# The last step of two layer norms on ScalarE instead of VectorE and GpSimd, in a kernel of windowed attention and product-key experts

## The chip, the cores and the metric

The kernel runs on one core of a Trainium2 chip. A core has five engines with an instruction queue of their own: PE (TensorE: matmuls and transposes), DVE (VectorE), ACT (ScalarE), POOL (GpSimd) and SP (SyncE, which here only issues DMAs). They run at the same time and wait for each other by semaphores. Each of them works through its queue in the order in which the program was built, so an instruction that waits holds up all those behind it. Tiles live in SBUF, matmul results in banks of PSUM.

The metric is the device time of one execution in microseconds (us). The kernel before took 1505.26 us, the median of 3 runs (1503.28 to 1505.82).

## The reference

The input x has 16 sequences (B) of 512 tokens (T) with 128 channels (D). Two residual layers are computed, each behind a layer norm without weights:

```python
def _layernorm(x, axis=-1, eps=1e-05):
    m = jnp.mean(x, axis=axis, keepdims=True)
    v = jnp.var(x, axis=axis, keepdims=True)
    return (x - m) / jnp.sqrt(v + eps)

x = L0_attn_x
x = x + _L0_attn_ref(_layernorm(x, axis=-1), L0_attn_w_qkv, L0_attn_w_proj)
x = x + _L0_ffn_ref(_layernorm(x, axis=-1), L0_ffn_gamma, L0_ffn_beta, L0_ffn_w_q,
                    L0_ffn_keys, L0_ffn_key_in, L0_ffn_key_out)
```

The attention has 16 heads of 8 channels. A token sees the tokens at most 128 places away:

```python
attn = jnp.einsum('bhqd,bhkd->bhqk', q, k) / math.sqrt(DK)
mask = jnp.abs(idx[None, :] - idx[:, None]) > WINDOW          # 128
p = jax.nn.softmax(jnp.where(mask[None, None], -1000000000.0, attn), axis=-1)
out = jnp.einsum('bhqk,bhkd->bhqd', p, v)                     # then the projection
```

The second layer normalises its input over all 8192 tokens, scores it against 2 x 8 x 32 keys, takes the eight best of each and the eight best of their sums, and weighs 1024 experts by them:

```python
mu, var = jnp.mean(x, axis=0), jnp.mean(jnp.square(x - mu), axis=0)
xn = (x - mu) * jax.lax.rsqrt(var + BN_EPS) * gamma + beta
sim = jnp.einsum('pbnhd,hkpd->pbnhk', (xn @ w_q.T)..., keys)
s, i = jax.lax.top_k(sim, 8)
o = jax.nn.gelu(inputs @ w_down) * jax.nn.softmax(scores, axis=-1)
out = jnp.einsum('bnhk,bnhkd->bnd', o, w_up)
```

## The kernel before

**Two stages.** An attention stage (up to about 716 us) is followed by an expert stage (to the end). The second cannot begin earlier, because its scores need mean and variance over all tokens: `bn_st` collects the statistics of each normalised sequence and L591 joins them. The change touches the attention stage alone.

**Attention.** The unit of work is a unit `n` of one sequence and four heads (64 in all), in four blocks `u` of 128 tokens. The outer loop (L548) runs over steps `s`, one step per (n, u). In a step, PE, DVE, ACT and POOL work on different units:

- `greatest` (L409) is two units ahead: a matmul of q with k into `s_ps` for each head, and on DVE a masked maximum over it (L424, written `masked` and `mx` in the profile). Four times a step. `s_ps` has three PSUM banks.
- `greatest_pieces` (on POOL, tiles `mr` and `mp`) and `greatest_rows` split the maxima into three bf16 pieces, transpose them on PE (`mT_ps`), copy them on ACT and write them by DMA into rows of `qst`, so that the next matmul subtracts them.
- `exponentials` (L453) is the unit itself: a matmul of k with q into `e_ps` for each head, and on ACT `Exp` of it into `pT` (L466). `e_ps` has three banks as well, so a matmul into `e_ps` waits for the Exp of the third one before it. POOL then zeroes the corners outside of the window (`affine_select`, called from L473).
- `weigh` (L479), two steps later: `pT` times v into `o_ps`.
- `divide` and `project` finish a unit and a sequence; L525 adds the result to `xs[b]`, which stays in SBUF for the whole kernel.

**Work beside it.** Three lines of steps run beside this loop, `preparing`, `ending` and `beside`, each a generator (`Steps`, L282). At the end of each step of the loop every line takes at most one step, and one that needs the single PSUM bank `ps_m` (it yields `BANK`) waits for a step in which that bank is free.

- `prepare(b)` (L339) makes q, k and v of a sequence three ahead: `normalised_T` (L320), which normalises the four blocks of 128 tokens into `xn`, transposes them on PE into `xn_ps` and copies them on ACT into `xnT`; then the matmuls, ACT's copies `qf` and `kf`, and POOL's splitting of q and k into bf16 pieces (`qp`, `kp`, `rest`).
- `second_norm(bs)` (L527) is the layer norm ahead of the experts: statistics, then `normalised_T` again with tiles called `xi`, `xi_ps` and `xiT`, and a DMA of `xiT` to DRAM. It runs in groups: sequences 0 to 5, 6 to 11, 12 and 13, 14, and 15 last (L547, L585).
- `ln_stats` (L303) makes the statistics of a group, block by block (`bn_stats` and `bn_aggr` on DVE), one step of the line for each sequence, and at the group's end one `Sqrt` on ACT and one reciprocal on DVE. For the first norm it is called for sequence 0, for 1, for 2 and 3, and for 4 to 15.
- `weights_of_experts` (L188) loads and prepares the experts' weights, behind the statistics of 4 to 15.

**Last step of a norm.** `normalised_T` computes (x - mean) x rstd for each of the four blocks by one instruction with two per-row operands. Of the four, the second and the fourth go to POOL, the others to DVE; for sequences 0 and 1 (first norm) and for the last sequence (second norm) all four go to DVE:

```python
alone = b == B - 1 if tag == "xi" else b < 2
what = (xn[:, t], xs[b][:, t], mv[:, t, 0:1], rstd[:, t : t + 1], ALU.subtract, ALU.mult)
if t % 2 and not alone:
    pool("tensor_scalar", *what)
else:
    nc.vector.tensor_scalar(*what)
```

The profile writes these as `xn<-x,mva,rsa` and `xi<-x,mvb,rsb`, at L330 for DVE and L172 (the helper `pool`) for POOL.

**What sets the order.** Matmuls, transposes and POOL's instructions in the helpers `mm`, `tr` and `pool` stay in the order of the program text. The others (ACT, DVE, memsets, DMAs) are placed by a planner when the program is built, by the costs that it assumes; on the chip each queue then runs in that fixed order. `Exp` and `Sqrt` need different tables on ACT, so a `Sqrt` between `Exp`s has an ACT_TABLE_LOAD on either side. The four square roots of the first norm stand ahead of the first `Exp`; those of the second norm lie among them.

Of the kernel before, what the change touches and what calls it, by code (L numbers as in the profile page):

```python
# [15 lines left out]
AF = mybir.ActivationFunctionType  # L16
ALU = mybir.AluOpType
# [26 lines left out]
def kernel(  # L44
# [13 lines left out]
    nc = tc.nc  # L58
    B, T, D = x.shape
    NH = 16  # L60
    DK = D // NH
    NQ = T // P
# [17 lines left out]
    xs = []  # L80
    for b in range(B):
        t = keep.tile([P, NQ, D], F32, name=f"x_{b}")
# [59 lines left out]
    def load(b):  # L142
        xts[b] = ahead.tile([P, T], F32, tag="xt", name=f"xt_{b}")
        nc.sync.dma_start(xts[b], xT[b])
# [8 lines left out]
    with ExitStack() as at:  # L153
# [12 lines left out]
        def mm(*args, **kw):  # L166

            tc.keep_in_program_order(nc.tensor.matmul(*args, **kw))  # L168

        def pool(op, *args, **kw):  # L170

            tc.keep_in_program_order(getattr(nc.gpsimd, op)(*args, **kw))  # L172

        def tr(out, in_, eye):
            tc.keep_in_program_order(nc.tensor.transpose(out, in_, eye))
# [12 lines left out]
        def weights_of_experts():  # L188

            for v in range(2):  # L190
                nc.sync.dma_start(
                    key_out_sb[v * NP : v * NP + NP], key_out.rearrange("(p c) d -> p c d", c=NC)
                )
            loads = [
                (f"key_in_{i}", key_in[4 * P * i : 4 * P * i + 4 * P].rearrange("(c p) d -> p c d", p=P))
                for i in range(2)
            ]
            loads.append(("keys", keys.rearrange("(c a) k p d -> (a k) c (p d)", c=2)))
            loads += [
                (f"w_q_{i}", w_q[4 * P * i : 4 * P * i + 4 * P].rearrange("(c k) d -> k c d", k=P))  # L200
                for i in range(4)
            ]
            raw = {}

            def fetch(i):
                if i < len(loads):
                    name, src = loads[i]
                    raw[i] = pw.tile([P, 4, D], F32, tag="raw", name=name)
                    dst = raw[i]
                    if name == "keys":  # L210
                        dst = dst.rearrange("q (c p) d -> q c (p d)", p=2)
                    nc.sync.dma_start(dst, src)

            fetch(0)
            fetch(1)
            yield
            yield
            yield BANK
            keysT = fix.tile([P, 2, 2, P], F32, name="keysT")
            for i in range(len(loads)):  # L220
                w = raw.pop(i)
                ps = ps_m.tile([P, 4, P], F32, tag="m", name=f"prep_ps_{i}")
                if i < 3:
                    for c in range(4):
                        tr(ps[:, c], w[:, c], ident)
                else:

                    for c in range(4):
                        s, h = divmod(4 * (i - 3) + c, H)
                        mm(  # L230
                            ps[:, c, 0:NK], lhsT=w[:, c],
                            rhs=keysT[:, h // 4, s, (h % 4) * NK : (h % 4 + 1) * NK],
                            start=True, stop=True,
                        )
                if i < 2:
                    nc.scalar.copy(
                        key_inT[:, :, NP // 2 * i : NP // 2 * i + NP // 2],
                        ps.rearrange("d k (p c) -> d c (k p)", c=NC),
                    )
                elif i == 2:  # L240
                    nc.scalar.copy(keysT.rearrange("p c s k -> p (c s) k"), ps)
                else:
                    s, h = divmod(4 * (i - 3), H)
                    nc.scalar.copy(
                        wsim.rearrange("p (h s k) -> p h s k", s=2, k=NK)[:, h : h + 4, s],
                        ps[:, :, 0:NK],
                    )
                fetch(i + 2)
                yield
                yield BANK if i + 1 < len(loads) else None  # L250
# [25 lines left out]
        pieced, attns, norms = {}, {}, {}  # L276
# [26 lines left out]
        def ln_stats(bs, name, into):  # L303

            n = len(bs) * NQ
            mv = ln.tile([P, n, 2], F32, tag=f"mv{name}{n}", name=f"mv{name}_{bs[0]}", bufs=3)
            for i in range(n):
                st = ln.tile([P, 6], F32, tag="st", name=f"st{name}_{bs[0]}_{i}", bufs=4)
                nc.vector.bn_stats(st, xs[bs[i // NQ]][:, i % NQ])
                nc.vector.bn_aggr(mv[:, i], st)  # L310
                if i % NQ == NQ - 1:
                    yield
            rstd = ln.tile([P, n], F32, tag=f"rs{name}{n}", name=f"rs{name}_{bs[0]}", bufs=3)
            nc.scalar.activation(rstd[:, 0:n], mv[:, 0:n, 1], AF.Sqrt, bias=eps)
            nc.vector.reciprocal(rstd[:, 0:n], rstd[:, 0:n])
            for i, b in enumerate(bs):
                into[b] = mv[:, i * NQ : i * NQ + NQ], rstd[:, i * NQ : i * NQ + NQ]
            yield

        def normalised_T(b, mv, rstd, dst, tag, then=None):  # L320

            xn = w2.tile([P, NQ, D], F32, tag="xn", name=f"{tag}_{b}")
            for t in range(NQ):

                alone = b == B - 1 if tag == "xi" else b < 2
                what = (xn[:, t], xs[b][:, t], mv[:, t, 0:1], rstd[:, t : t + 1], ALU.subtract, ALU.mult)
                if t % 2 and not alone:
                    pool("tensor_scalar", *what)
                else:
                    nc.vector.tensor_scalar(*what)  # L330
                if t % 2:
                    yield BANK if t == NQ - 1 else None
            ps = ps_m.tile([P, NQ, P], F32, tag="m", name=f"{tag}_ps_{b}")
            for t in range(NQ):
                tr(ps[:, t], xn[:, t], ident)
            nc.scalar.copy(dst, ps.rearrange("p t q -> p (t q)"))
            yield then
# [189 lines left out]
        def second_norm(bs):  # L527
            into = {}
            yield from ln_stats(bs, "b", into)
            for b in bs:  # L530
                t = w2.tile([P, T], F32, tag="xiT", name=f"xiT_{b}")
                yield from normalised_T(b, *into[b], t, "xi")
                nc.vector.bn_stats(bn_st[:, b], t)
                nc.sync.dma_start(xT[b], t)
# [7 lines left out]
        preparing, beside, ending = Steps(), Steps(), Steps()  # L542
# [5 lines left out]
        for s in range(-2 * NG * NQ, (NU + 1) * NQ):  # L548
            n, u = divmod(s, NQ)
            b, g = divmod(n, NG)  # L550
            if g == NG - 1 and u == 2 and b + 3 < B:
                preparing.rest()
                preparing.add(prepare(b + 3))
            if u == 0 and g == 1 and b == 0:
                beside.add(ln_stats(range(4, B), "a", norms), weights_of_experts())
            if u == 0 and g == 2 and b in groups:
                beside.add(second_norm(groups[b]))
            if u == 0 and g == 2 and b == B - 1:
                load(0)
                load(1)  # L560
            tops_of = greatest(n + AHEAD, u) if 0 <= n + AHEAD < NU else iter(())
            probs_of = exponentials(n, u) if 0 <= n < NU else iter(())
            next(tops_of, None)
            next(probs_of, None)
            next(tops_of, None)
            if 0 <= s - LATE < NU * NQ:
                weigh(*divmod(s - LATE, NQ))
            together(tops_of, probs_of)
            free = True
            if u == 0 and 0 <= n + AHEAD - 1 < NU:  # L570
                greatest_pieces(n + AHEAD - 1)
            if u == 1 and 0 <= n + AHEAD - 1 < NU:
                greatest_rows(n + AHEAD - 1)
                free = False
            if u == 2 and 0 <= n - 1 < NU:
                divide(n - 1)
                free = False
                if n % NG == 0:
                    ending.add(project(n // NG - 1))
                    ending.go(False)  # L580
            for steps in (preparing, ending, beside):
                free = steps.go(free)
            if u == NQ - 2 and 0 <= n + LAID < NU:
                lay(n + LAID)
# [41 lines left out]
    pe, dve, act, pool = (InOrder(e) for e in (nc.tensor, nc.vector, nc.scalar, nc.gpsimd))  # L626
# [333 lines left out]
    for i in range(NB):  # L960
        b, t = divmod(i, NQ)
# [110 lines left out]
```

## Time and profile before

| | |
|---|---|
| profiled execution | 1506.56 us, of which the span of the instructions is 1504.9 us |
| median of the runs shown | 1505.26 us |
| attention stage | 0 to about 716 us |
| start of attention, to the first `Exp` | 53.7 us |
| granted TensorE clock over the span | 0.984 |
| DVE, xn and xi by L330 | 36 x 499 ns mean, 34 x 482 ns mean |
| POOL, xn and xi by L172 | 28 x 806 ns mean, 30 x 801 ns mean |
| ACT, `Exp` at 384 and at 256 columns | 512 x 489 ns, 512 x 383 ns |
| ACT, table loads in attention | 11 x 1283 ns |

Busy time of an engine is the time in which it ran an instruction of its own. A row such as `A <- B: 8.8, 14, 0.9` in the list of waits says that A sat idle for 8.8 us in total, 14 times, at most 0.9 us, until B was done. In a list in order of time the columns are start and length in us, engine, line, operation, output and inputs with their shapes, how many in a row, and in brackets the idle time ahead and what ended it. `PEld` is the loading of weights into TensorE, beside the matmuls.

### The profile page before, as it was taken

The numbers are of one execution on the slowest core, as the hardware profiler recorded it, in microseconds if no ns is written. First come the engines' busy times: TensorE is split into PE (matmuls) and PEld (weight loads), VectorE is DVE, ScalarE is ACT, GpSimd is POOL, SyncE is SP. The second block draws the span as 40 slices with busy tenths as digits, with TensorE's granted clock in tenths as the row PEclk, the third lists the DMA queues.
The fourth block names the chain that finished last, engine by engine and source line by source line (L and its number), as shares of the span: only waits on it lengthen the run. The fifth ranks groups of instructions, "written<-read, shape, count | busy, mean of one in ns | idle before, by whom it ended". The sixth has DMA issues, their size and how long they took to land.

```text
span 1504.9 us, 48591 instructions
## 1 busy us (share of the span) xinstructions
PE 1395.0 (93%) x16880; PEld 844.1 (56%) x16880; DVE 1315.6 (87%) x7999; ACT 1212.4 (81%) x2596; POOL 1094.5 (73%) x1706
## 2 busy tenths in 40 slices
PE   3999999999999999896789999999999999999997
PEld 1445555544545545443456666666666666666666
DVE  6878888878888887882899999999999999999984
ACT  1577777777777777775889999999999999999963
POOL 8466666777777767563577887788878788788775
PEclk9999999999999999997999999999999999999989
DMA  6233332223333222320000000000000000000000
GB/s 177 86 111 101 102 94 84 85 79 89 92 91 92 86 85 76 101 63 36 10 9 10 9 17 10 16 17 9 16 10 17 17 10 16 10 16 10 10 2 24
DMA packets 53574, 74.96 MB, mean 50 GB/s; under 512 B 5840, under 2 KB 39888, under 8 KB 53200
## 3 DMA queue, kind: packets, MB, share of 16 engines
q1 hardware_dynamic: 52496, 71.59, 16.2%
q8 instruction: 134, 2.20, 0.6%
q14 instruction: 112, 0.92, 0.2%
q10 hardware_dynamic: 832, 0.26, 0.1%
HBM read 49.28 MB, written 20.97 MB: 47 GB/s over the span
## 4 chain that ended last, share of the span: by engine, by line
DVE 47%; PE 3%; issue 1%; ACT 1%; POOL 0%; ACTq 0%; POOLq 0%
DVE idx L624 10%; DVE row L624 9%; DVE place L624 6%; DVE top L624 6%; DVE mine L624 5%; DVE best L624 4%; DVE x_ps L624 3%; DVE num L624 2%; DVE upper L624 1%; PE up_ps L624 1%; DVE zs L624 1%; PE w_ps L624 1%; POOL cols L624 0%; PE dn_ps L624 0%; PE off_ps L624 0%
## 5 line engine op out<-in xcount | busy, mean ns | idle before, releaser
L424 DVE CUSTOM_DVE_ANT_0 masked<-s_ps,band 128x384 bf16<-128x384 f32 (+1 forms) x1024 | 459.1, 484 | 112.2 <-PE s_ps L168 95.7
L466 ACT ACTIVATE pT<-e_ps 128x384 f32<-128x384 f32 (+1 forms) x1024 | 389.4, 436 | 117.5 <-PE e_ps L168 111.1
L172 POOL TENSOR_SCALAR_AFFINE_SELECT pT<-pT 128x512 f32<-128x512 f32 x384 | 239.2, 639 | 188.8 <-ACT pT L466 187.2
L168 PE MATMUL s_ps<-kst,qst 128*128 128x384 bf16 (+1 forms) x1024 | 309.5, 307 | 22.2 <-DMA kst<-kv 11.0
L624 POOL TENSOR_TENSOR cols<-mine,wT 64x512 f32<-64x512 bf16 x256 | 270.0, 1055 | 25.7 <-ACT row L624 7.0
L624 PE MATMUL w_ps<-cols,row 128*64 128x32 f32 x8192 | 260.0, 224 | 13.6 <-POOL cols L624 13.6
L624 PEld LDWEIGHTS w_ps<-cols,row 128*64 128x64 f32 x8192 | 252.1, 139 | 32.3 <-POOL cols L624 27.8
L168 PE MATMUL e_ps<-qst,kst 128*128 128x384 bf16 (+1 forms) x1024 | 228.7, 302 | 13.1 <-ACT pT L466 12.4
L624 POOL TENSOR_TENSOR g<-g,gel 128x512 f32<-128x512 f32 x128 | 163.6, 1278 | 105.5 <-ACT g L624 105.5
L168 PEld LDWEIGHTS <-qst 128*128 128x128 bf16 x1024 | 100.5, 98 | 196.2 <-issue 168.4
L168 PE MATMUL o_ps<-pT,vaug 128*32 128x384 f32 (+1 forms) x2048 | 192.3, 447 | 0.4 <-POOL pT L172 0.4
L624 DVE FIND_INDEX8 idx<-top,sim 128x8 uint32<-128x32 f32 x1024 | 166.2, 185 | 0.0
L624 ACT ACTIVATE row<-off_p,one 128x512 f32<-128x512 bf16 x256 | 165.8, 749 | 0.0
L624 ACT ACT_TABLE_LOAD x122 | 156.5, 1283 | 2.2
L624 DVE TENSOR_TENSOR row<-x_ps,nums_p 128x1024 f32<-128x1024 f32 x128 | 150.0, 1213 | 0.0
L624 PE MATMUL up_ps<-g,key_out_sb 64*128 64x256 f32 (+2 forms) x1152 | 148.0, 384 | 0.0
L624 ACT ACTIVATE off_p<-off_ps 128x512 bf16<-128x512 f32 x256 | 132.4, 602 | 17.0 <-PE off_ps L624 16.8
L624 PE MATMUL dn_ps<-xt,key_inT 128*64 128x256 f32 x1024 | 125.6, 388 | 2.2 <-ACT sim L624 1.4
L168 PEld LDWEIGHTS <-kst 128*128 128x128 bf16 x1024 | 99.9, 98 | 45.4 <-issue 23.9
L624 PE MATMUL off_ps<-p_bf,ident_bf 128*128 128x512 bf16 x256 | 96.6, 377 | 19.7 <-ACT p_bf L624 19.6
L624 PEld LDWEIGHTS dn_ps<-xt,key_inT 128*64 128x64 f32 x1024 | 68.3, 137 | 78.3 <-ACT row L624 41.7
L624 DVE MAX8 top<-sim 128x8 f32<-128x32 f32 x1024 | 106.7, 177 | 2.9 <-ACT sim L624 2.9
(145 smaller groups left out, 2366.5 us busy)
## 6 DMA issues: line engine op xcount, KB each, us to landing
qst<-qv SPq DMA_DIRECT2D x192, 96.0 KB
kst<-kv SPq DMA_DIRECT2D x192, 96.0 KB
qv<-qp SPq DMA_DIRECT2D x16, 384.0 KB
kv<-kp SPq DMA_DIRECT2D x16, 384.0 KB
x<-in_L_attn_x_dram SPq DMA_DIRECT2D x16, 256.0 KB
xT<-xiT SPq DMA_DIRECT2D x16, 256.0 KB
xt<-xT SPq DMA_DIRECT2D x16, 256.0 KB
out_dram<-o_sb SPq DMA_DIRECT2D x16, 256.0 KB
```

Of the source, the lines that this page charges most:

```text
L168: tc.keep_in_program_order(nc.tensor.matmul(*args, **kw))
L172: tc.keep_in_program_order(getattr(nc.gpsimd, op)(*args, **kw))
L424: nc.vector.tensor_tensor_reduce(masked[h][:, 0:w], s, band.rearrange("p u k -> p (u k)")[:, from_u : from_u + w], 1.0, LOWEST, ALU.add, A ...
L466: nc.scalar.activation(pT[:, h, 0:w], e_ps[:, 0:w], AF.Exp)
L624: return lambda *args, **kw: tc.keep_in_program_order(op(*args, **kw))
```

## The change

The last step of both norms is written as x times rstd plus (-mean x rstd), and all four blocks of every sequence go to ACT as `Identity` with a per-row scale and a per-row bias. For the bias, `ln_stats` gets one more DVE instruction at a group's end, which overwrites the means by -mean x rstd. DVE and POOL have no part in that step any more.

`ln_stats` takes a step of its line after every two blocks of 128 tokens where it took one after four, so that a sequence's statistics are two steps.

The first norm's statistics of sequences 4 to 15 are made as two groups, 4 and 5, and 6 to 15, each with its own square root and reciprocal. `weights_of_experts` stays behind them.

```diff
@@ ln_stats @@
-                if i % NQ == NQ - 1:
+                if i % 2:
                     yield
             rstd = ln.tile([P, n], F32, tag=f"rs{name}{n}", name=f"rs{name}_{bs[0]}", bufs=3)
             nc.scalar.activation(rstd[:, 0:n], mv[:, 0:n, 1], AF.Sqrt, bias=eps)
             nc.vector.reciprocal(rstd[:, 0:n], rstd[:, 0:n])
+            nc.vector.scalar_tensor_tensor(
+                mv[:, 0:n, 0], mv[:, 0:n, 0], -1.0, rstd[:, 0:n], ALU.mult, ALU.mult
+            )
@@ normalised_T @@
-                alone = b == B - 1 if tag == "xi" else b < 2
-                what = (xn[:, t], xs[b][:, t], mv[:, t, 0:1], rstd[:, t : t + 1], ALU.subtract, ALU.mult)
-                if t % 2 and not alone:
-                    pool("tensor_scalar", *what)
-                else:
-                    nc.vector.tensor_scalar(*what)
+                nc.scalar.activation(
+                    xn[:, t], xs[b][:, t], AF.Identity, bias=mv[:, t, 0:1], scale=rstd[:, t : t + 1]
+                )
                 if t % 2:
                     yield BANK if t == NQ - 1 else None
@@ loop over steps @@
             if u == 0 and g == 1 and b == 0:
-                beside.add(ln_stats(range(4, B), "a", norms), weights_of_experts())
+                beside.add(ln_stats([4, 5], "a", norms), ln_stats(range(6, B), "a", norms))
+                beside.add(weights_of_experts())
```

## The prediction

> **What bounds the kernel now.** I read the page first, then a table of busy time by stretch, then the waits of PE between 60 and 700 us, then two places in order of time.
>
> The page's engine line, over the whole span:
>
> ```profile
> PE 1395.0 (93%) x16880; PEld 844.1 (56%) x16880; DVE 1315.6 (87%) x7999; ACT 1212.4 (81%) x2596; POOL 1094.5 (73%) x1706
> ```
>
> The edits touch only the attention stage, which ends at about 716 us; the expert stage after it issues the same instructions. Busy us of each engine in 10 us stretches (PE, PEld, DVE, ACT, POOL, then the granted clock):
>
> ```profile
> 320.00:330.00 10.00, 8.44 (x59) 4.86 (x61) 6.72 (x29) 7.63 (x18) 3.44 (x9) 0.83 0.18 51
> ...
> 350.00:360.00 10.00, 10.00 (x89) 5.65 (x89) 8.16 (x36) 7.41 (x19) 8.46 (x17) 1.00 0.25 74
> 360.00:370.00 10.00, 8.43 (x72) 4.66 (x71) 9.61 (x38) 7.17 (x18) 6.74 (x13) 1.00 0.39 118
> ```
>
> PE is full in an ordinary stretch, so attention lasts as long as PE's work and PE's stalls. Work taken from DVE or POOL is worth only the stalls it caused; work given to ACT costs only where PE comes to wait. What PE waited for from 60 to 700 us (total, times, longest):
>
> ```profile
> PE e_ps L168 <- ACT pT L466: 12.4, 6, 3.7
> PE s_ps L168 <- DVE mx L424: 8.8, 14, 0.9
> PE mT_ps L175 <- POOL mp L172: 5.0, 13, 0.6
> PE xi_ps L175 <- POOL xi L172: 1.0, 2, 0.8
> ```
>
> So at most about 10 us can be won from DVE and POOL. The third line isn't theirs: there POOL's chain follows a pT select that had waited for ACT (1.21 us idle at 173.6). A DVE stall and ACT's slack at one place, in order of time:
>
> ```profile
> 360.60 0.38 PE L168 MATMUL e_ps<-qst,kst 128*128 128x256 bf16 x2
> ...
> 360.69 0.59 ACT L336 COPY xiT<-xi_ps 128x512 f32<-128x512 f32 x1
> 360.69 1.92 DVE L330 TENSOR_SCALAR xn<-x,mva,rsa 128x128 f32<-128x128 f32 x2
> ...
> 361.17 0.67 ACT L466 ACTIVATE pT<-e_ps 128x256 f32<-128x256 f32 x2
> ...
> 361.93 0.38 PE L168 MATMUL e_ps<-qst,kst 128*128 128x256 bf16 x2
> ...
> 363.00 0.27 PE L168 MATMUL s_ps<-kst,qst 128*128 128x256 bf16 x1 [0.69 <-DVE mx L424]
> ...
> 365.05 0.32 PE L168 MATMUL s_ps<-kst,qst 128*128 128x384 bf16 x1 [0.88 <-DVE mx L424]
> ```
>
> And a square root in mid-stream, with its two table loads:
>
> ```profile
> 561.16 1.28 ACT L314 ACT_TABLE_LOAD   x1
> ...
> 562.67 0.32 ACT L314 ACTIVATE rsb<-mvb,eps 128x24 f32<-128x24 f32 x1 [0.23 <-DVE mvb L310]
> ...
> 563.00 1.28 ACT L466 ACT_TABLE_LOAD   x1
> 563.02 0.30 DVE L315 RECIPROCAL rsb<-rsb 128x24 f32<-128x24 f32 x1 [0.38 <-ACT rsb L314]
> ...
> 564.73 0.27 PE L168 MATMUL e_ps<-qst,kst 128*128 128x256 bf16 x1 [2.33 <-ACT pT L466]
> ```
>
> **The change, part by part.** It removes 70 TENSOR_SCALAR from DVE (36 xn, 34 xi) and 58 from POOL (28 and 30), and adds 128 Identity activations on ACT, ten small DVE instructions and one square root, which falls ahead of the first Exp. The changed program's order has as many table loads as before, so Identity brings none.
>
> *Price of one Identity.* The costliest ACT groups with pointer operands (busy us, mean ns), and four of the first in order of time:
>
> ```profile
> L624 ACT ACTIVATE row<-off_p,one 128x512 f32<-128x512 bf16 x256 | 165.8, 749 | 0.0
> L624 ACT ACTIVATE xb<-xt,bn_b,bn_a 128x512 f32<-128x512 f32 x16 | 13.0, 814 | 0.9 <-DVE bn_b L598 0.9
> ...
> 1005.24 2.59 ACT L624 ACTIVATE row<-off_p,one 128x512 f32<-128x512 bf16 x4
> ```
>
> The xb row is this very form at 512 columns: 814 ns. pT at 384 and 256 columns takes 489 and 383 ns, 0.83 ns a column, so 128 columns take 814 - 384 x 0.83 = 495 ns. Four of the Relu follow each other in 2.59 us, so the pitch is (2.59 - 0.749)/3 = 0.614, 0.135 below the duration; an Identity has a pitch of 0.36 us and four take 1.44. Ends: 0.17 (the 128x128 COPY, 266 ns, less the 0.1 by which a copy overlaps the next: 360.69 to 361.17 is 0.48 of 0.59) and 0.68 (xb whole). I take 0.36, the same form corrected for width. Together 46 us: ACT goes from 77% to 84% of 60-700 us.
>
> The Trainium skill, "ScalarE: Activation LUTs", section "What ACT_TABLE_LOAD costs", has 186 ns + 0.833 ns a column, 93 ns for each pointer operand and an overlap of 93 ns; an estimate from it is 479 ns, pitch 0.386, and the sum below would be 10.1 in place of 8.8. Its section "Rules for kernel authors" says to do add and mul on VectorE and not on ScalarE, which speaks against this change; that rule is about cost per element, and no row here gives the price of being queued ahead of Exp.
>
> *Bursts of four ahead of Exp.* In the changed order ten blocks have their four Identities between a copy (xiT, as at 360.69) and the next four Exp. e_ps has three banks. The second matmul of the pair at 361.93 started at 362.04 and needs the bank of the first of the pair at 360.60, whose Exp ended at 361.17 + 0.38 = 361.55; PE restarts 0.05 after an Exp. Slack 0.44. With 1.44 us more ahead of that Exp, PE stalls 1.0 us. Ten times: **+10.0** (by the two end pitches four take 0.66 and 2.7, less 0.44: 2.2 and 22.6). Behind PE's stalled matmul stand all its s_ps and o_ps.
>
> *Square roots.* In two of them (24 columns, at 319.5 and 562.7) ACT now goes sqrt, wait, four Identities, table load. The wait is DVE's reciprocal 0.30, the new instruction (about 0.25, between reciprocals of 4 and 24 columns at 0.18 and 0.30) and hand-overs, 0.75 in all. Behind the sqrt everything on ACT is queued, Exp first, and PE already stalls there, so all of 0.75 + 1.44 is added: 2 x 2.19 = **+4.4** (2.8 to 6.9). At the next two (636.2 and 678.8) four Identities stand ahead of the table load, but ACT waited 1.26 and 0.91 us for DVE's statistics, which cover most: +0.2 and +0.55, **+0.75** (0 to 3.3).
>
> *Clock.* After the stall at 319 the clock row reads 0.83 (1.7 us of ten lost); after the equal one at 563 it is 1.00. With stalls twice as long I count one more such loss: **+1.7** (0 to 3.4). The Trainium skill, "TensorE: Matmul & The Clock Gate", Part 1, says that a free-running window of 3.4 us without work halves the clock; by it the 2.3 us stalls are a matter of phase and 4.5 us ones always lose, so the sum stays as it is.
>
> *Single Identities.* Twelve blocks have them one, two, one between Exp pairs. ACT idles 0.17 to 0.6 us before most pairs; one fits, two (0.72) exceed 0.44 by little: **+1.0** (0 to 3).
>
> *Removed from DVE.* The 8.8 us are four places like 360-366 (0.69 + 0.88 each) and six of 0.41, all right behind TENSOR_SCALARs (1.92, or 1.04 us a pair), each longer than the stall: **-8.8** (-8.8 to -6.3). Next late there is ACT, counted above. POOL's 46 us lay in its waits for ACT (180 us).
>
> *Start.* ACT now runs block 1's four Identities before the copy of block 0's xnT (11.54 us before): statistics of blocks 2 and 3 end some 1 us sooner, their square root waits for block 0's Identities to 10.24, four more to 11.87: +0.35. POOL, full from 14.97 to the kp that the DMA at 28.07 waits for, loses an xn (0.81) and gets a memset (0.95) in its place: +0.15. **+0.5** (-0.8 to 1.5). SP's loads of expert weights come later among the qst loads, the same number; wsim was ready at 211 us and is needed at 716: nothing, and PE and ACT steps moved with them are as many.
>
> *End.* Steps of two blocks push one more xi transposition behind the last y_ps. xiT of block 13 takes block 14's place before the table load, block 14's copy goes behind the sqrt, then the last four Identities end at 712.25 where DVE ended at 711.60: +0.65. Ahead of it PE's waits for POOL's xi (0.83) and pT (0.36) go, and oT is no longer behind xiT: -1.5. **-0.8** (-1.5 to +0.7).
>
> Sum: 10.0 + 4.4 + 0.75 + 1.7 + 1.0 - 8.8 + 0.5 - 0.8 = **+8.8 us**. The profiled execution took 1506.56 us, 1.3 above the median; it goes to 1515.3, the median from 1505.26 to **1514.0**.
>
> **Rivals.**
> - *DVE's relief wins (faster).* If an Identity's pitch is a copy's 0.17, four take 0.66: bursts 2.2, square roots 2.8, no more clock loss, singles nothing. With -9.6 and +0.5 the sum is -4.1: 1501.2. It decides below a pitch of 0.19. For it: 16 us of DVE burst vanish where PE waited. Against: the xb and Relu rows.
> - *Slack is larger than one place shows (no change).* Exp pairs that wait 0.6 us for PE elsewhere; a stall of 0.4 a burst gives 4.0 for 10.0: 1508.0.
> - *ACT becomes the bound.* If half the single Identities also stall PE by 0.7 in each of the twelve blocks, 8.4 replaces 1.0: 1521.5. For it: ACT has no gap between oT and mT copies; against: 16% of the stage still idle.
>
> **How the numbers follow.** Forecast 0.61 (alone 1509 to 1519), faster rival 0.16, no change 0.13, ACT bound 0.10. About 0.2%, 3 us, is what a measurement here can tell from no change, so faster 0.16, same 0.13, slower 0.71. The sums of all low and all high ends are 1499 and 1540; 1503 to 1522 leaves out most of the first rival and the top of the last, two in ten.
>
> **What would show it.** Right: Identity near 495 ns; waits of s_ps for DVE mx near nothing; e_ps waiting for pT about 28 us in some sixteen places, those of 1 us behind an xiT copy; PE idle above 4 us at two square roots. Wrong: an Identity below 300 ns, or bursts with no stall behind them, or mT_ps waits that grow past 5 us, since POOL's chain stands behind ACT's pT.

## The result and the profile after

The changed kernel takes 1512.28 us, the median of 20 runs (1506.36 to 1516.22); the kernel before, run beside it, 1504.59 us (20 runs, 1501.97 to 1507.64). The ratio is 1.005, with a 95% interval of 1.0041 to 1.0058: 7.7 us slower, where 8.8 were forecast. The profiled execution took 1510.33 us (span 1508.6), 2 us below its median, and the one of before lay 2 us above its own; so the two traces differ by 3.8 us only; where the rest may lie is said below the table by stretch.

The page's engine line of the changed kernel: DVE and POOL gave up 24 and 49 us, ACT took 46, PE's work is the same.

```profile
PE 1392.5 (92%) x16880; PEld 842.0 (56%) x16880; DVE 1291.2 (86%) x7940; ACT 1258.6 (83%) x2725; POOL 1045.9 (69%) x1648
```

What PE waited for from 60 to 700 us in the changed kernel (total, times, longest; all rows). The row of `s_ps` for DVE's `mx` has gone whole, and the row of `e_ps` for ACT's `pT` has grown from 12.4 to 27.7 us.

```profile
PE e_ps L168 <- ACT pT L466: 27.7, 17, 4.6
PE mT_ps L175 <- POOL mp L172: 5.8, 16, 0.6
PE s_ps L168 <- DMA qst<-zeros: 1.5, 1, 1.5
```

Busy time by stretch (PE, PEld, DVE, ACT, POOL, then the granted clock, the DMA share and GB/s). PE was full from 350 to 370 us but for its waits for DVE; now it loses 0.94 us there to ACT. After the first square root the clock is 0.83 as before; in the stretch of the second, where it had been 1.00, it is 0.73.

```profile
320.00:330.00 10.00, 8.17 (x58) 4.59 (x61) 5.04 (x20) 7.62 (x18) 3.18 (x9) 0.83 0.05 18
350.00:360.00 10.00, 10.00 (x91) 5.66 (x88) 8.03 (x38) 7.41 (x19) 8.44 (x17) 1.00 0.24 73
360.00:370.00 10.00, 9.06 (x79) 5.05 (x81) 8.69 (x41) 8.92 (x24) 5.70 (x12) 1.00 0.39 120
560.00:570.00 10.00, 5.41 (x31) 3.09 (x29) 4.33 (x24) 7.47 (x16) 3.89 (x9) 0.73 0.29 88
```

One of the ten bursts, in order of time, at the place that the prediction showed of before. The four Identities run in one go behind the `xiT` copy, the next Exp starts at 362.79 in place of some 1.5 us earlier, and PE's matmul into the bank that this Exp frees waits 0.94 us.

```profile
360.67 0.38 PE L168 MATMUL e_ps<-qst,kst 128*128 128x256 bf16 x2
360.76 0.59 ACT L336 COPY xiT<-xi_ps 128x512 f32<-128x512 f32 x1
...
361.24 1.65 ACT L328 ACTIVATE xn<-x,mva,rsa 128x128 f32<-128x128 f32 x4
...
362.00 0.27 PE L168 MATMUL e_ps<-qst,kst 128*128 128x256 bf16 x1
...
362.79 1.18 ACT L466 ACTIVATE pT<-e_ps 128x256 f32<-128x256 f32 x4
...
363.21 0.27 PE L168 MATMUL e_ps<-qst,kst 128*128 128x256 bf16 x1 [0.94 <-ACT pT L466]
```

And the second square root in mid-stream. Between the root and the load of Exp's table stand the wait for DVE (0.59) and the four Identities; PE idles 4.56 us where it idled 2.33.

```profile
560.70 1.28 ACT L314 ACT_TABLE_LOAD   x1
...
562.20 0.32 ACT L314 ACTIVATE rsb<-mvb,eps 128x24 f32<-128x24 f32 x1 [0.22 <-DVE mvb L310]
562.54 0.30 DVE L315 RECIPROCAL rsb<-rsb 128x24 f32<-128x24 f32 x1 [0.38 <-ACT rsb L314]
562.88 0.18 DVE L316 SCALAR_TENSOR_TENSOR mvb<-mvb,rsb 128x24 f32<-128x24 f32 x1
563.10 1.65 ACT L328 ACTIVATE xi<-x,mvb,rsb 128x128 f32<-128x128 f32 x4 [0.59 <-DVE mvb L316]
564.77 1.28 ACT L466 ACT_TABLE_LOAD   x1
...
566.50 0.37 PE L168 MATMUL e_ps<-qst,kst 128*128 128x256 bf16 x1 [4.56 <-ACT pT L466]
```

At the third and the fourth root the stalls grew by little, because ACT's wait for DVE's statistics covers most of the four Identities there. First before, then after:

```profile
638.22 0.27 PE L168 MATMUL e_ps<-qst,kst 128*128 128x256 bf16 x1 [3.68 <-ACT pT L466]
...
680.80 1.07 PE L168 MATMUL e_ps<-qst,kst 128*128 128x256 bf16 x3 [3.66 <-ACT pT L466]
```

```profile
642.53 0.27 PE L168 MATMUL e_ps<-qst,kst 128*128 128x256 bf16 x1 [3.98 <-ACT pT L466]
...
687.69 1.07 PE L168 MATMUL e_ps<-qst,kst 128*128 128x256 bf16 x3 [4.31 <-ACT pT L466]
```

The 64 transpositions into `mT_ps`, one a unit, are marks at which two traces can be laid side by side. After minus before, by stretch (times of before):

| stretch | what lies in it | change, us |
|---|---|---|
| 0 to 57.4 | start | -2.3 |
| 57.4 to 312.8 | single Identities, loads of expert weights | +0.3 |
| 312.8 to 335.8 | first root | +2.0 |
| 335.8 to 556.0 | six bursts against nine waits for DVE | -0.5 |
| 556.0 to 577.4 | second root | +4.3 |
| 577.4 to 627.9 | two bursts against three waits for DVE | +0.15 |
| 627.9 to 670.8 | third root, two bursts | +2.2 |
| 670.8 to 683.8 | fourth root | +0.6 |
| 683.8 to 716.3 | end, to the experts' first `sim_ps` | -3.1 |

So the bursts and DVE's relief cancel almost exactly in the long middle, and the roots are the loss. In the row of the second root 2.2 of the 4.3 us are the longer wait; the clock lost 3.4 us more there (one minus the granted share, summed over 4 us windows), part of it while PE stood still. The two negative rows at the ends lie where the clock was lost in the profile of before: 3.4 us between 40 and 60 us, where after lost nothing, and 6.8 against 1.7 between 700 and 724 us. At the start x also arrived 0.56 us earlier in the second profile. That these make up the two rows is likely, not shown. From 60 to 700 us all rows of PE's waits add up to 35.0 us after and 28.3 before, 6.7 us more, next to the 7.7 of the medians.

### The profile page after: what moved, and what is told of

Read it like the earlier page. It is cut to its first block, busy times and chain, and to the rows that moved or that the text cites. A ratio compares the mean times of both kernels' runs of the same rounds, so it can differ in the third digit from the quotient of the medians.

```text
span 1508.6 us, 48606 instructions
## 1 busy us (share of the span) xinstructions
PE 1392.5 (92%) x16880; PEld 842.0 (56%) x16880; DVE 1291.2 (86%) x7940; ACT 1258.6 (83%) x2725; POOL 1045.9 (69%) x1648
## 4 chain that ended last, share of the span: by engine, by line
DVE 48%; PE 38%; ACT 6%; POOL 4%; issue 2%; DMA 2%; SPq 1%; POOLq 0%; ACTq 0%
DVE idx L625 10%; PE o_ps L168 10%; PE s_ps L168 9%; DVE row L625 9%; PE e_ps L168 8%; DVE place L625 6%; DVE top L625 6%; DVE mine L625 5%; DVE best L625 4%; DVE x_ps L625 3%; ACT pT L466 2%; DVE num L625 2%; PE t_ps L175 2%; PE mT_ps L175 1%; DVE upper L625 1%
## 5 line engine op out<-in xcount | busy, mean ns | idle before, releaser
L168 PE MATMUL e_ps<-qst,kst 128*128 128x384 bf16 (+1 forms) x1024 | 230.5, 302 | 28.4 <-ACT pT L466 27.7
```

## Experiments

Each kernel was timed in several rounds beside the kernel before, which took 1505.0 to 1505.8 us in these jobs. Theory A is that of the prediction: an instruction on ACT costs what it makes the next Exp late by, less a slack.

**Which part of the change: e1 and e2.** The steps undone, or done alone:

```diff
 # e1: the changed kernel, with
-                if i % 2:
+                if i % NQ == NQ - 1:
                     yield
-                beside.add(ln_stats([4, 5], "a", norms), ln_stats(range(6, B), "a", norms))
-                beside.add(weights_of_experts())
+                beside.add(ln_stats(range(4, B), "a", norms), weights_of_experts())
 # e2: the kernel before, with the same lines the other way round
```

> The changed kernel with its step changes undone: statistics yield once a block and blocks 4 to 15 are one group, ahead of the expert weights, as before; the norms' last step is still Identity on ACT. Theory A (what I predicted from: the Identities queued ahead of Exp cost the time, DVE's relief gives 8.8 us back, the steps are worth next to nothing): the order of ACT has the same ten fours behind an xiT copy and the same four behind a square root, so e_ps waits for pT about 27 us between 60 and 705 us, s_ps for DVE mx near nothing, and the 1.5 us wait for the load of qst from zeros at 132 us is gone, since the expert weights are loaded where they were before: about 1511 us (1508 to 1513). Rival B (the finer steps and the later loads of the expert weights lose the time, Identity is even): 1504 to 1506 us, as the kernel before.

> The kernel before with the step changes alone: statistics yield every two blocks of 128, blocks 4 and 5 are a group of their own, and the expert weights come behind all statistics; the norms' last step stays a TENSOR_SCALAR on DVE and POOL. Theory A: s_ps waits for DVE mx stay near 8.8 us and e_ps for pT near 12.4 us; added is the 1.5 us wait for qst from zeros near 132 us: about 1506 us (1503.5 to 1508). Rival B (the steps and the moved loads are the loss): 1510 to 1513 us.

e1 took 1514.18 us, ratio 1.0054 (1.0041 to 1.0068); e2 1505.64 us, ratio 1.000 (0.9989 to 1.0011). The waits from 60 to 700 us, first of e1, then of e2:

```profile
PE e_ps L168 <- ACT pT L466: 27.0, 15, 4.6
PE mT_ps L175 <- POOL mp L172: 5.8, 16, 0.6
PE s_ps L168 <- DMA qst<-mT: 1.3, 1, 1.3
...
```

```profile
PE e_ps L168 <- ACT pT L466: 12.9, 7, 3.7
PE s_ps L168 <- DVE mx L424: 8.8, 14, 0.9
PE mT_ps L175 <- POOL mp L172: 5.8, 15, 0.6
PE s_ps L168 <- DMA qst<-mT: 1.7, 1, 1.7
...
```

The whole loss is Identity's. The finer steps move one wait for `qst` from 112 us (0.6 to 1.3 us long in the six profiles with the old steps) to about 140 us (1.5 to 2.1 in seven of the eight with the new; e3 has no such wait), and the time does not show it.

**Price and slack: e5 and e6.** Two Identities in place of four, and eight.

```diff
 # e5: the changed kernel, with
+                if t % 2:
                     nc.scalar.activation(xn[:, t], xs[b][:, t], AF.Identity, ...)
+                else:
+                    nc.vector.tensor_scalar(xn[:, t], xs[b][:, t], rstd..., mv..., ALU.mult, ALU.add)
 # e6: the changed kernel, with
+                for _ in range(2):
                     nc.scalar.activation(xn[:, t], xs[b][:, t], AF.Identity, ...)
```

> The changed kernel with half of its Identities given back: of each block's four, t = 1 and 3 stay on ACT (where POOL had them in mid-stream) and t = 0 and 2 go to DVE as TENSOR_SCALAR; POOL has none. Ten times two Identities stand behind an xiT copy, and two behind each of the four square roots. Theory A (the price is what stands ahead of Exp, less a slack): four took 4 x 0.387 = 1.55 us of ACT and cost 0.94, so the slack is 0.61 and two (0.77) cost 0.16: the ten waits go from 9.4 us in all to 1.6, and each of the four root waits falls by 0.77, to about 3.8, 3.8, 3.2 and 3.5. The waits of s_ps for DVE mx come back only in part (0 to 3 us), because a TENSOR_SCALAR pair took 1.0 to 1.9 us in the kernel before with POOL busy on the same work, and POOL has none now: 1502.5 us (1499 to 1506). Rival B (each engine's total is the bound; what ACT is spared DVE loses): the 8.8 us of waits for DVE mx come back whole: 1508 to 1511 us.

> The changed kernel with each Identity done twice into the same place (256 in place of 128, 49.5 us more on ACT). In its order eight stand behind an xiT copy in the ten places, eleven times two and then, past a qf copy, three more stand ahead of one Exp, and at the square roots eight or four. Theory A (slack 0.61 ahead of each group of Exp, what exceeds it is paid): the ten waits go from 0.94 to 2.49 us, +15.5; the eleven cost (1.94 - 0.61) about 1 us each, +11; the roots +1.5 to 6; the clock lost after some of the longer stalls +2 to 6; pairs elsewhere +0.2 each: 1545 us (1532 to 1555). Rival R3 (ACT is the bound already: every us on it is a us of time): 49.5 us more, 1562 us. Rival R2 (much larger slack outside the ten places): the ten and the roots alone, 1528 to 1532 us.

e5 took 1511.13 us, ratio 1.0042 (1.0029 to 1.0056); e6 1558.57 us, ratio 1.0347 (1.0333 to 1.0361). One burst of each, in order of time: e5 at the place of the burst shown above, then e6.

```profile
363.06 1.84 DVE L333 TENSOR_SCALAR xn<-x,rsa,mva 128x128 f32<-128x128 f32 x2
...
364.66 0.27 PE L168 MATMUL e_ps<-qst,kst 128*128 128x256 bf16 x1 [0.17 <-ACT pT L471]
...
365.29 0.27 PE L168 MATMUL s_ps<-kst,qst 128*128 128x256 bf16 x1 [0.36 <-DVE mx L429]
...
367.34 0.32 PE L168 MATMUL s_ps<-kst,qst 128*128 128x384 bf16 x1 [0.88 <-DVE mx L429]
```

```profile
376.83 0.27 PE L168 MATMUL e_ps<-qst,kst 128*128 128x256 bf16 x1 [2.48 <-ACT pT L467]
```

Behind two, four and eight Identities the trace has waits of 0.17, 0.94 and 2.48 us: 0.385 for each one more, which is the pitch ((1.65 - 0.489)/3 = 0.387), behind a slack of 0.60. That much of theory A holds to 0.02 us. Both times lie outside theory A's ranges, and e5's is the rival's (1508 to 1511). In e5 the waits for DVE came back more than expected, 5.0 us: a pair of TENSOR_SCALAR on DVE still took 1.84 us there although POOL had none (POOL ran its splitting of k and its masks beside it), and the 0.88 stands behind the statistics that follow. That is not all. Its waits from 60 to 700 us add up to 28.7 us, as much as the 28.3 of the kernel before, yet it is 5.3 us slower than that kernel in the same job. What differs is the clock: 0.979 in the mean of its five runs against 0.984 in that kernel's, so that 32 us of the span were lost and not 24.5. Not all lost clock shows in the time, so the 5.3 us are not accounted for to the last. One sequence, four units, takes 41.02 us in the changed kernel (from the wait at 363.21 to the one at 404.23), 41.08 in e5 and 41.07 in the kernel before: three ways of doing the step, one price where the clock is full. In e6 the stalls of 2.48 us also cost clock: 10.2 us were lost between 348 and 548 us, 1.7 behind each of six, where the changed kernel lost none. That fits what lies above 1545. By its time alone e6 is nearer to R3 (1562); but ACT was busy in 523 of the 640 us from 60 to 700 us, about as in the changed kernel (521), and so was not full.

**The roots: e9 and e4.** e9 gives the second norm of sequences 0, 6, 12 and 14, the first of each group, back to DVE and POOL; e4 keeps all on ACT and takes the root away.

```diff
 # e9: the changed kernel, with
+                if tag == "xn" or b not in (0, 6, 12, B - 2):
                     nc.scalar.activation(xn[:, t], xs[b][:, t], AF.Identity, ...)
+                elif t % 2:
+                    pool("tensor_scalar", ...)
+                else:
+                    nc.vector.tensor_scalar(...)
 # e4: the changed kernel, with
-            nc.scalar.activation(rstd[:, 0:n], mv[:, 0:n, 1], AF.Sqrt, bias=eps)
+            nc.vector.tensor_scalar(rstd[:, 0:n], mv[:, 0:n, 1], 1.0, EPS, ALU.mult, ALU.add)
             nc.vector.reciprocal(rstd[:, 0:n], rstd[:, 0:n])
```

> The changed kernel with the second norm of blocks 0, 6, 12 and 14, the first of each group behind a square root in mid-stream, given back to DVE (t = 0, 2) and POOL (t = 1, 3); the other blocks stay on ACT. Behind the two roots of 24 columns ACT then goes root, table load, Exp, as in the kernel before. Theory A (what the roots cost more than before is the wait for DVE's reciprocal and product and the four Identities, 2.23 us each): the two waits of 4.56 us go back to 2.33, together -4.5; one wait of 0.94 goes with block 12; the clock loss of 3.4 us behind the root at 566 us goes wholly or by half, since in the kernel before the clock was full there: 1505.5 us (1503 to 1508.5). Rival (the roots' waits only shift work that waits elsewhere): above 1509 us.

> The changed kernel without the norms' square roots: DVE adds eps and takes the reciprocal of the variance itself, so that ACT has neither the root nor its two table loads, and what is computed is a different norm (the root is left out; all else is done). It measures what the roots cost in mid-stream. Theory A (all of ACT's time at a root lies on the path): the four waits of 4.6, 4.6, 4.0 and 4.3 us go down to that of a plain four, 0.9 us or less, 14 to 17 us, and the clock losses behind them go too (1.7 to 3.4 us); at the end one table load of 1.3 us goes: 1494 us (1490 to 1499). Rival (the roots cover other waits, which come up in their place, DVE's statistics or POOL's masks): a gain below 8 us, 1504 us or more.

e9 took 1504.61 us, ratio 1.0002 (0.9992 to 1.0012): with four of 32 norms given back the loss is gone within the interval, as expected. Its two first roots, and one of the bursts that stayed:

```profile
320.00 0.27 PE L168 MATMUL e_ps<-qst,kst 128*128 128x256 bf16 x1 [2.32 <-ACT pT L473]
...
359.77 0.27 PE L168 MATMUL e_ps<-qst,kst 128*128 128x256 bf16 x1 [0.94 <-ACT pT L473]
...
560.83 0.27 PE L168 MATMUL e_ps<-qst,kst 128*128 128x256 bf16 x1 [2.32 <-ACT pT L473]
```

Waits explain 5.0 of the 7.7 us between the medians of the changed kernel and e9 (2 x 2.24 and one burst of 0.94, less a wait for DVE of 0.41 that came back at 657.71). For the other 2.7 there is only the clock to name: behind these two roots it lost 0 and 1.7 us in e9's profile against 1.7 and 3.4, and over all runs its mean is 0.986 against 0.983. How much of it is time is not shown.

e4 took 1504.85 us, ratio 0.9991 (0.9981 to 1.0001), 7.4 us less than the changed kernel and not the 18 of theory A; the rival had it. At the third and fourth root the waits fell to 0.94 and 1.27, but at the first two 3.15 us stayed. ACT and DVE there, in order of time:

```profile
317.19 0.66 ACT L466 ACTIVATE pT<-e_ps 128x256 f32<-128x256 f32 x2 [0.60 <-PE e_ps L168]
...
319.03 0.30 DVE L310 BATCH_NORM_AGGREGATE mvb<-stb 128x2 f32<-128x6 f32 x2
...
320.30 1.65 ACT L328 ACTIVATE xi<-x,mvb,rsb 128x128 f32<-128x128 f32 x4 [2.45 <-DVE mvb L316]
321.85 1.20 ACT L466 ACTIVATE pT<-e_ps 128x256 f32<-128x256 f32 x4
...
322.26 0.37 PE L168 MATMUL e_ps<-qst,kst 128*128 128x256 bf16 x1 [3.15 <-ACT pT L466]
```

The planner put the Identities ahead of Exp, and now they, not the root, wait in ACT's queue for the last statistics. A table load had hidden that wait.

**Can the root go elsewhere: e7 and e8.** e7 is the kernel before with its four mid-stream roots worked out on DVE; e8 adds this to e5, with sequences 0, 6, 12 and 14 (the first of each group) wholly on DVE in both norms.

```diff
+            half, s = (var + eps) / 2, half + 0.5          # one tensor_scalar each
+            for _ in range(4):
+                nc.vector.reciprocal(r, s)
+                nc.vector.tensor_tensor(r, r, half, ALU.mult)
+                nc.vector.scalar_tensor_tensor(s, s, 0.5, r, ALU.mult, ALU.add)
+            nc.vector.reciprocal(r, s)
```

> The kernel before, with its four square roots in mid-stream (groups of 24, 24, 8 and 4 columns) worked out on DVE: a first guess (1 + v)/2 and four steps s = s/2 + v/(2s), fifteen small instructions in place of one reciprocal, so that ACT has no root and no table load there; all else as before, the norms' last step on DVE and POOL. Nothing of ACT waits for the statistics then. Theory A (a root costs its two table loads and what ACT waits for in between, as the 2.33, 2.33, 3.68 and 3.66 us of waits for pT say): 12.0 us go, and the clock loss behind them (1.7 to 3.4 us); DVE's fifteen, about 0.2 us each, give back 0 to 1.5 us a group in waits for mx: 1494 us (1490 to 1499). Rival (what the table loads hid comes out in their place, as it did where the changed kernel was run without roots and two waits of 3.15 us stayed): 1500 to 1504 us. The difference between the two kernels is whether an instruction of ACT has to wait for DVE's statistics.

> The changed kernel with two Identities on ACT and two TENSOR_SCALAR on DVE a block (as in the half run), the four mid-stream roots on DVE in fifteen small instructions, and the first block of each group wholly on DVE, so that ACT never waits for statistics in mid-stream. Theory A: the ten places cost 1.6 us in all, the roots nothing but DVE's own delay (0 to 6 us in all), POOL's share of the norms is gone: 1490 us (1486 to 1497), below both kernels. Rival (DVE, with fifteen instructions and all of a first block, becomes what PE waits for, 2 us or more in each of the four places, and half of the 8.8 us comes back): 1498 to 1503 us.

Both expectations fell, and both times lie above the rivals' ranges too: e7 1509.04 us, ratio 1.0022 (1.0011 to 1.0033); e8 1507.40 us, ratio 1.0021 (1.0012 to 1.0031). In e7 `e_ps` waits for `pT` went from 12.4 to 0.2 us, and `s_ps` for `mx` from 8.8 to 22.2; in e8, where the rival had named DVE, the latter are 21.2 us. Rows of e7, then DVE's queue there, and PE:

```profile
PE s_ps L168 <- DVE mx L439: 22.2, 17, 4.9
...
PE e_ps L168 <- ACT pT L481: 0.2, 1, 0.2
```


```profile
318.56 0.34 DVE L307 TENSOR_SCALAR hv<-mvb 128x24 f32<-128x24 f32 x1
...
322.34 0.30 DVE L313 RECIPROCAL rsb<-sd 128x24 f32<-128x24 f32 x1
...
323.67 0.32 PE L168 MATMUL s_ps<-kst,qst 128*128 128x384 bf16 x1 [4.26 <-DVE mx L439]
```

The fifteen ran in one piece from 318.56 to 322.64, 4.1 us, ahead of the maxima that free PE's banks. No wait of ACT came out in the table loads' place, as e7's rival had it: the chain itself, in DVE's queue, made PE wait 13.4 us at three of the roots (4.26, 4.26 and 4.93), where the roots on ACT had made it wait 12.0 at all four.

**Spreading the Identities: e3.** One Identity a step, and ACT held to the written order:

```diff
-                if t % 2:
-                    yield BANK if t == NQ - 1 else None
+                yield BANK if t == NQ - 1 else None
 # and every ACT instruction from the first Exp on:
+            tc.keep_in_program_order(...)
```

> The changed kernel with its Identities taken apart: normalised_T hands back after each one, not after two, and ACT runs its instructions in the order in which they are written, so that no more than one Identity (in fifteen places two with a copy between) stands ahead of the next Exp, and none directly behind a square root. All Identities are still there, and ACT is as busy. Theory A: a single Identity, 0.39 us of pitch, fits into the slack of 0.44, so the ten waits of 0.94 us for pT vanish (9.4 us), and of the four square roots' waits (4.6, 4.6, 4.0, 4.3) about 1.4 to 2.2 us each: 1498 us (1494 to 1505), below both kernels, unless the written order puts a copy ahead of Exp where the planner had put it behind. Rival R3 (ACT's total of busy time is the bound, not where the Identities stand): no change, 1511 to 1514 us.

It took 1523.36 us, ratio 1.0118 (1.01 to 1.0137), above the ranges of both theories. Its waits from 60 to 700 us:

```profile
PE mT_ps L182 <- POOL mp L172: 11.6, 30, 1.0
PE v_ps L168 <- ACT mT L175: 10.0, 12, 0.8
PE e_ps L168 <- ACT pT L175: 8.3, 5, 2.5
PE s_ps L168 <- DVE mx L431: 6.2, 12, 0.9
```

The waits of `e_ps` did fall, from 27.7 to 8.3, as theory A has it; the written order brought new ones, 0.83 us twelve times behind the `mT` copy above all. And with more steps a norm, four transpositions of `xi` were left for after the last `y_ps`: from there to `sim_ps` it took 18.9 us (712.63 to 731.48) against 11.5. Order and steps were changed in one run, so what each is worth is not told apart.

**What the step costs at all, and a better split: e11, e10 and e12.** e11 is the kernel before without the step. e10 and e12 are the kernel before with one and two of the four on ACT, where no root stands ahead.

```diff
 # e11: the kernel before, with
-                tr(ps[:, t], xn[:, t], ident)
+                tr(ps[:, t], xs[b][:, t], ident)              # and no tensor_scalar
 # e10, e12: the kernel before, with -mean x rstd in place of the mean, and
+                elif t in (2,):                               # e12: (0, 2)
+                    nc.scalar.activation(xn[:, t], xs[b][:, t], AF.Identity, ...)
                 elif t % 2:
                     pool("tensor_scalar", ...)
```

> The kernel before without the norms' last step: x itself is transposed, no engine subtracts the mean and multiplies by the root's reciprocal (statistics and roots are still made, nothing reads them). It measures what the step cost where DVE and POOL did it, and so the most that any move of it can give back. Theory A (in the attention stage the TENSOR_SCALARs cost the waits behind them and no more): from the mT transposition at 57 us to the last one at 684 us, s_ps waits for DVE mx go from 8.8 to nothing and POOL's xi waits with them, e_ps keeps its 12.4 at the roots: 8 to 10 us less in that stretch. At the start the first block no longer waits for its statistics (2 to 3 us less), at the end neither does the last (3 to 4 us less): 1490 us in all (1486 to 1494). Rival (the 16 us of burst on DVE and 46 us on POOL are hidden but for part of the 8.8): 5 us or less in the stretch, 1494 to 1498 in all.

> The kernel before with one of each block's four 128x128 of the norms' last step on ACT as Identity (t = 2), one on DVE (t = 0) and two on POOL (t = 1 and 3) as TENSOR_SCALAR with multiply and add; the first blocks behind square roots, blocks 0 and 1 and the last as before; steps as before. Theory A (slack of 0.61 us ahead of Exp, and DVE's waits come from a pair of TENSOR_SCALAR in one go): one Identity, 0.39 us, costs nothing in the ten places, +0.4 at two of the roots; with one TENSOR_SCALAR in place of two DVE is 0.96 us less behind in each place, so the six waits of 0.41 us go, the four of 0.69 go, and the four of 0.88, which stayed in the half run behind the statistics, stay or shrink: s_ps waits 0 to 3.6 us in place of 8.8: 1500 us (1497 to 1503). Rival (what DVE waits for is POOL's use of what they share, whatever the count on DVE): waits of s_ps above 6 us, 1503 to 1506 us.

> As the three-engine run, with two of four on ACT (t = 0 and 2), two on POOL and none on DVE, but for the first blocks behind roots, blocks 0 and 1 and the last. Theory A (slack of 0.61 ahead of Exp; without TENSOR_SCALAR DVE is not late): ten e_ps waits of 0.17 us come, 1.7 in all, the s_ps waits of 3.6 us go, and two of the roots' waits grow by 0.4 each: 1500.5 us (1498 to 1503), no further from the three-engine run than can be measured. Rival (s_ps waits of 0.6 stay, since the statistics of the next group alone make DVE late there): 1502 to 1505 us.

e11 took 1489.78 us, ratio 0.9901 (0.9885 to 0.9916); between the marks at 57 and 684 us it is 10.3 us shorter than before, and the row of `s_ps` for `mx` is gone. e10 took 1501.54 us, ratio 0.9965 (0.995 to 0.998), e12 1498.02 us, ratio 0.9954 (0.9941 to 0.9968): both beat the kernel before in the same job, and with it the changed one, and are not told apart from each other. Waits from 60 to 700 us, e10, then e12:

```profile
PE e_ps L168 <- ACT pT L477: 11.7, 5, 3.4
PE mT_ps L175 <- POOL mp L172: 4.6, 14, 0.6
PE s_ps L168 <- DVE mx L435: 3.6, 10, 0.6
...
```

```profile
PE e_ps L168 <- ACT pT L477: 13.4, 15, 3.5
PE mT_ps L175 <- POOL mp L172: 5.8, 18, 0.6
...
```

One Identity fits into the slack; two make PE wait 0.17 us, in nine places of e12; and the waits for DVE fall to 3.6 us and, in e12, to a single one of 0.41 us, at the tenth place (653.87).

## Why the prediction was right, point by point

| term | forecast, us | measured |
|---|---|---|
| ten bursts | +10.0 | 10 x 0.94 = +9.4 |
| first two roots | +4.4 | 2 x (4.56 - 2.33) = +4.5 |
| third and fourth root | +0.75 | 0.30 + 0.65 = +0.95 |
| clock | +1.7 | 0 and 3.4 us more lost behind the first two roots; the time that this cost is not shown |
| single Identities | +1.0 | nothing |
| DVE and POOL relieved | -8.8 | -8.8, the row is gone |
| start | +0.5 | first `s_ps` 33.29 us after the first statistics, 33.25 before: 0 |
| end | -0.8 | -3.1 in the profiles, with 5.1 us less clock lost: open |

The mechanism was right, and so was the total, but the total is right in part by luck: singles and start were put at 1.5 us too much, and the clock is not known to its 1.7.

**Bursts.** The wait is 0.94 and not 1.0 by two errors that cancel. The pitch is 0.387 and not 0.36, so four take 1.55 and not 1.44 us; the slack, as the waits show it, is 0.60 and not 0.44. (An estimate from the figures of the Trainium skill, "ScalarE: Activation LUTs", section "What ACT_TABLE_LOAD costs", was 0.386; the trace agrees.) Part of the second difference is one of counting. The prediction counted from the time at which the stalled matmul would have started, 0.11 us after the one ahead; the trace counts a wait from the end of that one, which took 0.27 (362.00 to 362.27, and 0.94 more is 363.21). In time a burst costs a little over the wait: e11, which has none, takes 38.91 us for a sequence (342.49 to 381.40 between marks) where the changed kernel with two takes 41.02, so 1.05 each, and the slack by that count is 0.50.

**Roots.** Right to 0.1 us, and for the reason given: e9 takes the Identities from behind them and the waits go back to 2.32. Here too two errors cancel: the wait for DVE is 0.59 and not 0.75, and the four Identities take their whole 1.65 and not 1.44, since the table load behind them does not overlap the last. That nearly the whole loss sits here was not said; the prediction set the bursts' 10.0 against DVE's 8.8 term by term, and of the places of DVE's waits it says only "Next late there is ACT, counted above", not that the bursts come at the same ten, so that one takes the place of the other.

**Singles.** The twelve sequences with one, two and one between Exp pairs cost nothing: of the 27.7 us, 9.4 are bursts, 17.4 the four roots, and the rest lies at 696 to 700 us. The slack there holds two.

**Not foreseen.** Three of the bursts late in the stage have a wait of `mT_ps` for POOL's `mp` behind them, 0.58 to 0.59 each (in the list 5.8 against 5.0 us): POOL's chain, later by the stall, ends last there. It was named as a sign of being wrong ("mT_ps waits that grow past 5 us") and given no term; taken by the letter, 0.8 us of the account went against it. The -1.0 of POOL's `xi` is there. DVE got eleven small instructions and not ten, because the added square root has a reciprocal of its own.

**Rivals.** DVE's relief is all that it could be (8.8 us, and 10.3 with what else the step costs, by e11) and still loses. The no-change case with a stall of 0.4 a burst is out: each is 0.94. ACT is not the bound: in e10 and e12 it is busy 10 and 18 us longer than before (1222.0 and 1230.3 against 1212.4 us), and both are faster.

## What to carry to other kernels

Work moved to an engine with time to spare costs what it delays in that engine's queue, at the place where it lands: count the instructions between the last event and the next one that the bottleneck waits for, multiply by the pitch, and take off the slack, which is best measured by putting two and four times the work there. An instruction that waits for another engine must not stand in the queue ahead of what the bottleneck needs; a table load or a root may hide that wait until it is removed. Spread a burst over the engines so that each stays near its own slack: here two of four on ACT and two on POOL (e12, ratio 0.9954) beat two on DVE and two on POOL (before) and four on ACT, even where those do not stand behind the first two roots (e9, 1.0002), although the Trainium skill, "ScalarE: Activation LUTs", section "Rules for kernel authors", sends such work to VectorE; in this stage the measurement decides otherwise.

## What the runs showed of the hardware that was not expected

- Granted clock is lost in quanta. Summed over 4 us windows, the loss behind one stall of PE is 0, 1.7 or 3.4 us in all the cases below. Behind the ten stalls of 0.94 us: none. Behind twelve stalls of 2.32 us (the first two roots of six kernels: before, e2, e9, e10, e11, e12): 1.7 in nine, 0 in three. Behind ten of 2.48 us in e6: 1.7 in nine, 0 in one. Behind six of 3.79 and 4.56 us (the first two roots of the changed kernel, e1 and e5): 1.7 once, 3.4 five times. But behind the third root's stall of 3.68 or 3.98 us (before, e2, e5, the changed kernel, e1, e9) it was 1.7 all six times, and behind six of 4.26 to 4.93 us in e7 and e8 1.7 five times and 3.4 once: the length of a stall alone does not tell the loss. The Trainium skill, "TensorE: Matmul & The Clock Gate", Part 1, tells of a free-running window of about 3.4 us and half the rate, which fits 1.7 as half of one; but its section "HAM oscillation" warns of idle gaps above 3.4 us, and here gaps of 2.3 to 2.5 us lost a quantum eighteen times in twenty-two. The prediction took from Part 1 that a stall of 2.3 us is a matter of phase and one of 4.5 always loses; a window of 3.4 us without work does not fit into the first, and into the second only in some phases, so this does not follow from the page.
- The times of the changed kernel follow the mean clock: its fastest run, 1506.36 us, had 0.988, the two slowest, 1515.20 and 1516.22 us, had 0.977. Over the span that is 18 us of clock lost against 35, and 9 to 10 us of time: in these three runs some half of the lost clock shows in the time.
- A pair of 128x128 TENSOR_SCALAR in fp32 on DVE took 1.84 us beside POOL's other work in e5, as much as the 1.92 us in the kernel before, where POOL ran such instructions too; at the start, with POOL waiting, four took 1.09 us.
